# A two-layer graph network on one core: the second layer by node, the first layers a batch behind, and the last layers but one inside the last sums

## The chip, the cores and the metric

The kernel runs on one core of a Trainium2 chip. The metric is device time in microseconds (us) of one execution, the median of several runs. Five engines work side by side, each on its own queue of instructions: PE (TensorE, matrix products; PEld is its weight load), DVE (VectorE), ACT (ScalarE), POOL (GpSimd) and SP (SyncE, which here issues DMAs). In a product `matmul(ps, stationary, moving)` the stationary operand is loaded and the moving one is streamed through it. PSUM is the memory that PE writes to, in banks of 512 float32 columns; SBUF is the memory of the other engines. All waits between engines are semaphores that the framework's scheduler derives from the data.

## What is computed

There are 6250 nodes with 64 features, and 206250 directed edges (src, dst), sorted by dst: 100000 random pairs in both directions and a loop at each node. Cut to what matters:

```python
def gin_conv(x, Wa, ba, Wb, bb):
    h = x + segment_sum(x[src], dst, N)
    return relu(h @ Wa + ba) @ Wb + bb
def gnn0(h):                                   # 64 -> 128 -> 128, 128 -> 128 -> 64
    h = relu(gin_conv(h, W1, b1, W2, b2))
    return gin_conv(h, W3, b3, W4, b4)
def gnn1(h):
    y = mlp3(h[src], WM1, bM1, WM2, bM2, WM3, bM3)      # a message of each edge
    z = segment_sum(y, dst, N)
    return mlp3(concat([h, z]), WU1, bU1, WU2, bU2, WU3, bU3)
x = x + gnn0(maximum(layernorm(x), 0))
x = x + gnn1(maximum(layernorm(x), 0))
```

Messages depend on the source alone, so all three segment sums are products with one matrix A of edge counts, A[src, dst].

## The kernel before

The nodes are cut into 49 tiles of 128. The function `fast` (L152) has three stages.

**Stage 1, about 0 to 388 us: A is built, and the first sum is made beside it.** For each tile of destinations, `build` (L395) makes one-hot matrices of the tile's edges on DVE (`hot` L376: there L383, high L387, low L390), and PE multiplies them in four rounds of 16 products with 49 columns (cnt, L406). ACT takes each round from PSUM into `a` as counts (L408), and SP stores the tile to A in DRAM (L412). After each round, `build` calls `between(i)` (L533). That does a quarter of the first sum of the tile before (`FirstSum.quarter` L511: 49 products of 195 columns with the tile's counts as stationary and `hp`, the normalised nodes, as moving, L514, and one with the identity, L517). `hp` is kept as three bf16 parts of 64 features, and each part has one more column, of ones or zeros, whose sum counts the edges. A reduction on DVE (L520) adds the parts into `r1`.

`between` also runs what the table `beside` (L459 to L474) sets for this quarter: the preparation of later batches of edges. A batch has two chunks of edges; 13 batches cover the tiles, so one batch serves four tiles. The steps of a batch are `search_block` (ACT, L307, L309), `fetch_edges` (L312: DVE computes the addresses `off`, L318, and POOL issues the indirect DMAs d_win and s_win, L322), `fetch_blocks` (POOL, blk, L297), `slots` (L328, some ten small DVE operations on the lists, among them pair L341, mine L346, high_i L349), `cast` (ACT L364) and `turn` (PE L372, ACT L374).

After every fourth tile, `first_layers` (L523) copies the counted column to `sums` on POOL (L526) and calls `conv1` (L444) for the four tiles: `by_feature` (L415) splits r1 into two fp32r halves vr (ACT L251, DVE L252), turns them with four PE transposes tf (L421), and ACT brings them to f (L424). `layer` (L427) multiplies by the two halves of W1 (ps_t1, two products of 512 columns), ACT adds the bias and applies ReLU (t1, L433). The second layer is one fp32 product with w2 stationary and t1 moving (ps_t2, 512 columns), again with bias and ReLU on ACT. The features are on the partitions now, so four transposes tb (L450) bring the nodes back there, and `halves` writes h2r, the two fp32r halves of the hidden nodes (ACT L251, DVE L252). All pieces follow each other at once in the program, so PE meets each with as much other work between as the scheduler's order has placed.

The preparation of the edges runs up to four batches ahead. `follow` (L273) places an instruction behind the newest count on its engine without a wait.

**Stages 2 and 3, two calls of `sweep` (L620).** The groups are eleven of four tiles, one of three and one of two. For each group, SP loads A's columns in 13 chunks of four source tiles (a<-A, L629), DVE or ACT widens the bytes to fp32r (ar, L633), and PE sums over all 49 source tiles: in stage 2 two products for each (both halves of h2r, 98 in all, 512 columns), in stage 3 one (yr holds both halves). The layers that follow a group, conv2 (L592) and conv3 (L608), are called once the next group's sums have been issued (L642 to L644), and those of the last group after the loop (L645). `conv3` ends with o (L614) and its stores to the output (L617); the last group's output is two DMAs, a full tile and one of 106 rows, both on SP. `weight_halves` (L255) splits W1, WM1 and WU1 into fp32r halves after the second tile has been built (L546), all under one name.

The pools of stage 1 are closed at L552, and those of the sweeps (L553 to L557) take their place in memory.

Of the kernel before, what the change touches and what calls it, by code (L numbers as in the profile page):

```python
# [42 lines left out]
P = 128  # L43
N = 6250
E = 206250
D = 64
# [24 lines left out]
FIRST_HOTS = ((0, 16), (16, 16), (32, 32))  # L71
XT = 7
# [24 lines left out]
class Params:  # L97


    def __init__(self, nc, const, W1, b1, W2, b2, W3, b3, W4, b4,  # L100
# [31 lines left out]
        self.e1, self.e2, self.q3 = column(bU1, "e1"), column(bU2, "e2"), row(bU3, "q3")  # L132
        self.eps = const.tile([P, 1], FP, name="eps")
# [18 lines left out]
def fast(ctx: ExitStack, tc: tile.TileContext, x, src, dst, w, bad, out):  # L152
# [24 lines left out]
    w.load(nc.sync)  # L177

# [33 lines left out]
    D1 = D + 1  # L212
    hp = once.tile([P, NT, NP, D1], BF, name="hp")
# [8 lines left out]
    sums = const.tile([P, NT], FP, name="sums")  # L222

# [16 lines left out]
    def split(parts, v, n, f):  # L240

        p1, p2, p3 = (parts[:, :, i, :f] for i in range(NP))
# [12 lines left out]
    def weight_halves(w):  # L255

        t = const.tile([P, 1, 2, HID], FR, name="wp")
        follow(halves(t, w[:, None, :]), "ACT")
        return [t[:, 0, i, :] for i in range(2)]


    wins = building.enter_context(tc.tile_pool(name="f_wins", bufs=2))
    hots = building.enter_context(tc.tile_pool(name="f_hots", bufs=2))
    amat = building.enter_context(tc.tile_pool(name="f_amat", bufs=3))
# [150 lines left out]
    def by_feature(v, n, scale=1.0, to=None):  # L415

        vr = work.tile([P, 4, 2, D], FR, name="vr")[:, :n]
        halves(vr, v)
# [6 lines left out]
        return to  # L425

# [17 lines left out]
    def conv1(t, n, r):  # L444
        f = by_feature(r[:, :n, :D], n, UNIT)
        t1 = layer(w.c1, n, "t1", *((part, f) for part in w1p))
        t2 = layer(w.c2, n, "t2", (w.w2, t1))
        ps = bank("tb")
        for j in range(n):
            nc.tensor.transpose(ps[:, j * P:(j + 1) * P], t2[:, j * P:(j + 1) * P], w.ident)  # L450
        halves(h2r[:, t:t + n], ps[:, :n * P].rearrange("p (t f) -> p t f", f=HID))
# [23 lines left out]

    for b in range(4):
        search(b)
    for i in range(NP):
        nc.gpsimd.memset(hp[:, :, i, D:], 1.0 if i == 0 else 0.0)
# [22 lines left out]
    r1 = {}  # L502

    class FirstSum:


        def __init__(self, t, a):
            self.t, self.a = t, a.bitcast(F8)
            self.acc = pacc.tile([P, CH], FP, name="acc")[:, :NP * D1]

        def quarter(self, i):  # L511
            t = self.t
            for k in range((H * i + 3) // 4, (H * (i + 1) + 3) // 4):
                nc.tensor.matmul(self.acc, self.a[:, k, :], hp[:, k].rearrange("p i d -> p (i d)"),  # L514
                                 start=(k == 0), stop=False)
# [14 lines left out]
    for t in range(NT + 2):  # L530
# [19 lines left out]
        if t >= 2:  # L550
            first_layers(t - 2)
# [348 lines left out]
```

## Time and profile before

| | us |
|---|---|
| three runs | 938.75, 940.83, 939.69 (median 939.69) |
| the profiled execution | 936.85, its span 935.1, clock 0.99 |
| PE busy | 867.9 |
| DVE busy | 623.4 |
| ACT busy | 583.7 |
| POOL busy | 143.1 |

The profile is of one execution, slightly faster than the three timed runs. In its groups, `x2401 | 247.8, 251` means 2401 instructions, busy for 247.8 us together, with a mean of 251 ns for one; matmuls are pipelined and overlap each other, so on PE the time from one start to the next is what one costs, and the sum of durations is more than that. An fp32 product shows as two records (passes), an fp32r or bf16 product as one. `[2.44 <-DMA a<-A]` at the end of a line of the timeline is idle time of the engine before the instruction, and what ended it. In windows, the columns are the busy time (and the instructions) of PE, PEld, DVE, ACT and POOL, then the clock granted to PE, the share of the DMA engines and GB/s.

### The profile page before, as it was taken

Reading aid. Unit: us, or ns where it says so; the run is one execution under the profiler, and the core shown is the slowest. Engines: PE = TensorE matmul, PEld = TensorE weight load, DVE = VectorE, ACT = ScalarE, POOL = GpSimd, SP = SyncE. Lnnn points to the kernel's source line nnn. Section 1 sums busy time; section 2 is a strip of 40 time slices with the busy share of each in tenths; the row PEclk is TensorE's granted clock in tenths of the full one; section 3 lists DMA queues with packets and bytes.
Section 4 is the critical chain, followed back from the end, with each engine's and each line's share of the span. In section 5 each row is a group of like instructions: output and inputs, shape, how many; then the busy total and the mean of one; then the engine's idle time right before and its main releaser. Section 6 shows DMA issues by size and latency. Waiting matters only on the chain.

```text
span 935.1 us, 19639 instructions
## 1 busy us (share of the span) xinstructions
PE 867.9 (93%) x8225; PEld 732.1 (78%) x8225; DVE 623.4 (67%) x927; ACT 583.7 (62%) x757; POOL 143.1 (15%) x101
## 2 busy tenths in 40 slices
PE   0279999999999999899999999999999989999995
PEld 0179999999999999877777787777789757777784
DVE  6899988889998898544455554445545656665651
ACT  5967776777776666544545554544545857777762
POOL 3654333445332410000000000000000000000000
PEclk9989999999999999999999999999999989999998
DMA  6234333443423323655444444444434748887861
GB/s 133 82 133 169 148 136 140 156 160 138 169 114 123 145 105 127 195 139 142 113 115 120 123 105 123 118 114 116 111 92 121 208 135 225 224 228 209 239 180 47
DMA packets 195671, 133.71 MB, mean 143 GB/s; under 512 B 35220, under 2 KB 186900, under 8 KB 195572
## 3 DMA queue, kind: packets, MB, share of 16 engines
q1 hardware_dynamic: 189236, 121.34, 44.0%
q0 software_dynamic: 3600, 10.32, 3.6%
q8 instruction: 66, 1.08, 0.5%
q10 hardware_dynamic: 2736, 0.69, 0.3%
q14 instruction: 33, 0.27, 0.1%
HBM read 91.38 MB, written 40.94 MB: 142 GB/s over the span
## 4 chain that ended last, share of the span: by engine, by line
PE 81%; ACT 9%; DMA 4%; DVE 3%; issue 1%; SPq 0%; POOL 0%; ACTq 0%; DVEq 0%
PE acc L640 41%; PE acc L514 20%; PE ps_t L431 8%; PE cnt L406 6%; PE ps_y L440 4%; DMA a<-A 3%; ACT a L408 2%; ACT ar L633 2%; ACT t L433 2%; PE tf L421 1%; PE tb L450 1%; ACT blk L307 1%; ACT f L424 1%; ACT junk L287 1%; DMA xs<-in_x_dram 1%
## 5 line engine op out<-in xcount | busy, mean ns | idle before, releaser
L633 DVE CAST ar<-a 128x2048 fp32r<-128x2048 uint8 (+2 forms) x208 | 220.1, 1072 | 201.9 <-PE acc L640 160.0
L633 ACT CAST ar<-a 128x2048 fp32r<-128x2048 uint8 (+2 forms) x130 | 234.5, 1805 | 140.6 <-PE acc L640 121.9
L640 PE MATMUL acc<-ar,h2r 128*128 128x512 f32 (+2 forms) x1274 | 303.4, 391 | 2.4 <-DMA a<-A 2.4
L640 PEld LDWEIGHTS acc<-ar,h2r 128*128 128x128 f32 x1274 | 229.9, 188 | 56.7 <-issue 13.7
L514 PE MATMUL acc<-hp,a 128*128 128x195 bf16 x2401 | 247.8, 251 | 4.5 <-ACT a L408 2.9
L514 PEld LDWEIGHTS <-a 128*128 128x128 fp8e4 x2401 | 200.8, 99 | 12.5 <-issue 6.9
L408 ACT ACTIVATE a<-cnt 128x784 int16<-128x784 f32 x196 | 160.8, 821 | 68.7 <-PE cnt L406 67.6
L640 PE MATMUL acc<-ar,yr 128*128 128x512 f32 (+2 forms) x637 | 158.4, 400 | 0.1
L640 PEld LDWEIGHTS acc<-ar,yr 128*128 128x128 f32 x637 | 115.7, 189 | 32.9 <-issue 10.4
L406 PE MATMUL cnt<-high,low 128*128 128x49 bf16 x3136 | 114.9, 187 | 12.6 <-DVE low L390 11.1
L406 PEld LDWEIGHTS <-low 128*128 128x128 fp8e4 x3136 | 108.1, 97 | 17.2 <-DVE low L390 11.6
L390 DVE TENSOR_TENSOR low<-there,lkw 128x2048 int32<-128x2048 bf16 (+2 forms) x51 | 112.1, 2197 | 0.0
L387 DVE TENSOR_TENSOR high<-high,lkw 128x3136 bf16<-128x3136 bf16 (+2 forms) x51 | 87.6, 1719 | 5.2 <-PE cnt L406 5.0
L383 DVE TENSOR_TENSOR there<-word,lkw 128x2048 bf16<-128x2048 bf16 (+2 forms) x51 | 59.1, 1176 | 0.0
L297 POOL DMA_INDIRECT blk<-in_dst_dram,row x25 | 37.0, 1478 | 130.6 <-ACT junk L309 108.5
L322 POOL DMA_INDIRECT s_win<-in_src_dram,off x25 | 41.8, 1674 | 7.6 <-issue 7.3
L322 POOL DMA_INDIRECT d_win<-in_dst_dram,off x25 | 39.0, 1560 | 8.4 <-issue 5.8
L433 ACT ACTIVATE t<-ps_t,c 128x512 f32<-128x512 f32 (+3 forms) x39 | 25.9, 663 | 19.9 <-PE ps_t L431 18.7
L526 POOL COPY sums<-r 128x4 f32<-128x4 f32 (+1 forms) x13 | 22.7, 1743 | 101.0 <-DVE r L520 100.9
L372 PE MATMUL ps_win<-identb,parts 128*128 128x128 bf16 x75 | 8.9, 225 | 16.5 <-ACT parts L364 16.5
L433 ACT ACTIVATE t<-ps_t,d 128x512 f32<-128x512 f32 (+2 forms) x26 | 17.2, 662 | 11.0 <-PE ps_t L431 11.0
L520 DVE TENSOR_REDUCE r<-acc 128x65 f32<-128x195 f32 x49 | 17.3, 354 | 5.6 <-PE acc L517 5.6
(123 smaller groups left out, 618.0 us busy)
## 6 DMA issues: line engine op xcount, KB each, us to landing
a<-A SPq DMA_DIRECT2D x264, 256.0 KB, 3.1
A<-a SPq DMA_DIRECT2D x49, 784.0 KB, 3.5
a<-A SPq DMA_DIRECT2D x24, 192.0 KB, 2.6
a<-A SPq DMA_DIRECT2D x24, 128.0 KB, 2.2
a<-A SPq DMA_DIRECT2D x22, 64.0 KB, 2.2
out_dram<-o SPq DMA_DIRECT2D x11, 128.0 KB, 2.0
xs<-in_x_dram ACTq DMA_DIRECT2D x3, 224.0 KB, 5.5
xs<-in_x_dram SPq DMA_DIRECT2D x3, 224.0 KB, 6.1
```

What stands on the lines that cost most here:

```text
L322: nc.gpsimd.indirect_dma_start(out=win[:, i, :], out_offset=None, in_=of.rearrange("(a o) -> a o", o=1), in_offset=bass.IndirectOffsetOnAx ...
L383: nc.vector.tensor_tensor(there, word2[:, None, :, :].to_broadcast(shape), of(0)[:, :, None, :].to_broadcast(shape), op=OP.is_equal)
L387: nc.vector.tensor_tensor(high, high2[:, None, :, :].to_broadcast(shape), of(1)[:, :, None, :].to_broadcast(shape), op=OP.is_equal)
L390: counted["DVE"] = nc.vector.tensor_tensor(low.rearrange("p (g i) w -> p g i w", i=2), there.rearrange("p g w i -> p g i w"), of(2)[:, :, ...
L406: counted["PE"] = nc.tensor.matmul(ps[:, b, j * H:(j + 1) * H], low[:, g, :], high[:, g // 2, :, g % 2], start=True, stop=True)
L408: counted["ACT"] = nc.scalar.activation(a[:, :, k:k + 2 * PG].rearrange("p h (b j) -> p h b j", b=2), ps[:, :, :PG * H].rearrange("p b (j ...
L431: nc.tensor.matmul(ps[:, :n * P], wt, rhs, start=(i == 0), stop=(i == len(terms) - 1))
L433: nc.scalar.activation(to, ps[:, :n * P], AF.Relu, bias=bias)
L440: nc.tensor.matmul(ps[:, j * D:(j + 1) * D], lhs[:, j * P:(j + 1) * P], wt, start=True, stop=True)
L514: nc.tensor.matmul(self.acc, self.a[:, k, :], hp[:, k].rearrange("p i d -> p (i d)"), start=(k == 0), stop=False)
L633: widen(ar.rearrange(f"p k t b -> {order}"), a.rearrange(f"p t (k b) -> {order}", b=P))
L640: nc.tensor.matmul(acc[:, :n * P], part, ar[:, k - k0].rearrange("p t b -> p (t b)"), start=(k == 0 and i == 0), stop=(k == H - 1 and i == ...
```

## The change

Five things are edited.

1. *Second layer by node.* t1 is now the stationary operand, four times 128 columns, and w2 the moving one, so that the result has the nodes on the partitions. The bias is then along the columns, and a product of ones (2 x 128) with a row c2_r (2 x 512, the bias in two halves that add up) starts the sum in PSUM. ACT writes h2r's first half with a ReLU, DVE the second with a maximum and a difference. The transposes tb and the operation t2 are gone. c2_r takes one more DMA and some operations after the second tile.
2. *A batch behind.* `conv1` is split into first_halves, first_turn, first_layer and second_layer. These enter `beside`: in the second quarter of the tiles 4g+5, 4g+6 and 4g+7, with the second layer of the group before beside the first layer of the next. The last two groups, and group 10's second layer, follow the loop, interleaved.
3. *First sums.* `hp` has one column of ones for all parts, 193 columns in all, and two tiles share a PSUM bank. Both are reduced together after the second, and ACT, not POOL, takes `sums` from PSUM.
4. *Pools.* The pool of `a` is the first of the inner ones; the halves of W1 are in a pool of stage 1, those of WM1 and WU1 have names of their own.
5. *End.* In each sweep, the layers of the last group but one are called at the fifth chunk of the last group's sums. The last 106 output rows go out on ACT's queue.

```diff
+MIXED = (NT - 8) // 4 + 1
...
+    c2_row = once.tile([2, HID], FP, name="c2_row")
+    nc.sync.dma_start(c2_row, w.b2.rearrange("(o f) -> o f", o=1).broadcast_to([2, HID]))
...
-    D1 = D + 1
-    hp = once.tile([P, NT, NP, D1], BF, name="hp")
+    HP = NP * D + 1
+    hp = once.tile([P, NT, HP], BF, name="hp")
...
+    amat = building.enter_context(tc.tile_pool(name="f_amat", bufs=3))
     wins = building.enter_context(tc.tile_pool(name="f_wins", bufs=2))
     hots = building.enter_context(tc.tile_pool(name="f_hots", bufs=2))
-    amat = building.enter_context(tc.tile_pool(name="f_amat", bufs=3))
...
-    def conv1(t, n, r):
-        f = by_feature(r[:, :n, :D], n, UNIT)
-        t1 = layer(w.c1, n, "t1", *((part, f) for part in w1p))
-        t2 = layer(w.c2, n, "t2", (w.w2, t1))
-        ps = bank("tb")
+    def first_halves(g):
+        n = group(g)[1]
+        vr1[g] = work.tile([P, 4, 2, D], FR, name="vr")[:, :n]
+        follow(halves(vr1[g], r1[g][:, :n, :]), "ACT")
+
+    def first_turn(g):
+        f1[g] = turned(vr1.pop(g), group(g)[1], UNIT)
+
+    def first_layer(g):
+        f = f1.pop(g)
+        t1s[g] = layer(w.c1, group(g)[1], "t1", *((part, f) for part in w1p))
+
+    def second_layer(g):
+        t, n = group(g)
+        t1 = t1s.pop(g)
+        ps = bank("ps_h")
+        nc.tensor.matmul(ps[:, :n * HID], ones_r, c2_r[:, :n * HID], start=True, stop=False)
         for j in range(n):
-            nc.tensor.transpose(ps[:, j * P:(j + 1) * P], t2[:, j * P:(j + 1) * P], w.ident)
-        halves(h2r[:, t:t + n], ps[:, :n * P].rearrange("p (t f) -> p t f", f=HID))
+            nc.tensor.matmul(ps[:, j * HID:(j + 1) * HID], t1[:, j * P:(j + 1) * P], w.w2, start=False,
+                             stop=(j == n - 1))
+        v = ps[:, :n * HID].rearrange("p (t f) -> p t f", f=HID)
+        nc.scalar.activation(h2r[:, t:t + n, 0, :], v, AF.Relu)
+        nc.vector.scalar_tensor_tensor(h2r[:, t:t + n, 1, :], v, 0.0, h2r[:, t:t + n, 0, :],
+                                       op0=OP.max, op1=OP.subtract)
...
+    for g in range(MIXED):
+        for u, what, of in ((5, first_halves, g), (6, first_turn, g), (7, first_layer, g), (7, second_layer, g - 1)):
+            if of >= 0:
+                beside.setdefault(4 * (4 * g + u) + 1, []).append((what, (of,)))
...
-            self.acc = pacc.tile([P, CH], FP, name="acc")[:, :NP * D1]
+            if t % 2 == 0:
+                acc1[t // 2] = pacc.tile([P, CH], FP, name="acc")[:, :2 * HP].rearrange("p (t d) -> p t d", d=HP)
...
+                nc.tensor.matmul(acc[:, t % 2, :], ident_a, hp[:, t], start=False, stop=True)
+                if t % 2 == 1 or t == NT - 1:
+                    t0, n = t - t % 2, t % 2 + 1
+                    if t0 % 4 == 0:
+                        r1[t // 4] = work.tile([P, 4, D], FP, name="r1")
+                    for j in range(n):
+                        nc.vector.tensor_reduce(r1[t // 4][:, t0 % 4 + j, :],
+                                                acc[:, j, :NP * D].rearrange("p (k d) -> p d k", k=NP),
+                                                axis=AX.X, op=OP.add)
+                    follow(nc.scalar.copy(sums[:, t0:t0 + n], acc[:, :n, NP * D]), "ACT")
-
-    def first_layers(t):
-        if t % 4 == 3 or t == NT - 1:
-            t0, n = t - t % 4, t % 4 + 1
-            nc.gpsimd.tensor_copy(sums[:, t0:t0 + n], r1[t // 4][:, :n, D])
-            conv1(t0, n, r1[t // 4])
...
-                w1p, m1p, u1p = (weight_halves(x) for x in (w.w1x, w.m1x, w.u1x))
+                w1p = weight_halves(w.w1x, "w1p", once)
+                m1p, u1p = weight_halves(w.m1x, "m1p"), weight_halves(w.u1x, "u1p")
+
+                hi = once.tile([2, 2, HID], FR, name="c2_halves")
...
-        if t >= 2:
-            first_layers(t - 2)
+    for what, g in ((second_layer, MIXED - 1), (first_halves, MIXED), (first_turn, MIXED), (first_halves, MIXED + 1),
+                    (first_layer, MIXED), (first_turn, MIXED + 1), (second_layer, MIXED), (first_layer, MIXED + 1),
+                    (second_layer, MIXED + 1)):
+        what(g)
...
+                queue = nc.sync if m == P else nc.scalar
...
+                if (t, n) == GROUPS[-1] and c == 4:
+                    then(*pending)
+                    pending = None
```

`turned` is the second half of the old `by_feature`, from its transposes on.

## The prediction

> **What bounds the kernel now.** I read the page's busy rows first, then windows of 50 us, the timeline of each engine through one period of four tiles, DVE's waits, and both ends of the stages.
>
> ```profile
> PE 867.9 (93%) x8225; PEld 732.1 (78%) x8225; DVE 623.4 (67%) x927; ACT 583.7 (62%) x757; POOL 143.1 (15%) x101
> ```
> ```profile
> 200.00:250.00 50.00, 49.58 (x865) 46.81 (x864) 43.97 (x53) 35.73 (x57) 19.60 (x12) 1.00 0.37 140
> ```
>
> PE is the bound by the page. The window of stage 1 (columns: PE, PEld, DVE, ACT, POOL) says so too, but DVE is busy 43.97 of 50 there: two engines are near the end of their time. PE's timeline prices a first layer:
>
> ```profile
> 253.27 0.60 PE L421 MATMUL tf<-ident,vr 128*128 128x128 f32 x4
> ...
> 254.55 0.74 PE L431 MATMUL ps_t<-f,wp 128*128 128x512 f32 x2
> ...
> 256.07 1.13 PE L431 MATMUL ps_t<-t,w 128*128 128x512 f32 x2
> ...
> 257.97 0.66 PE L450 MATMUL tb<-ident,t 128*128 128x128 f32 x4
> ...
> 262.32 0.58 PE L406 MATMUL cnt<-high,low 128*128 128x49 bf16 x16
> ...
> 268.30 0.33 PE L372 MATMUL ps_win<-identb,parts 128*128 128x128 bf16 x3
> ```
>
> The tile that begins at 253.27 takes 9.05 us, the next, with no layers, 5.98: the layers cost PE 3.07 in each period. The ps_t with t as its moving operand, the second layer, comes at 90.70, 118.25 ... 311.28, so a period is 27.55 us.
>
> DVE's own loop is almost as long. Each period it sends out an address list (off), and later takes the gathered list (high_i):
>
> ```profile
> DVE high_i L349 <- DMA s_win<-in_src_dram,off: 20.1, 8, 3.9
> ```
> ```profile
> 224.44 0.15 DVE L318 TENSOR_SCALAR off<-off_f 128x2 int32<-128x2 f32 x1
> ...
> 235.26 0.29 DVE L349 TENSOR_SCALAR high_i<-s_win 128x256 int32<-128x256 int32 x1 [2.10 <-DMA s_win<-in_src_dram,off]
> ...
> 251.47 0.15 DVE L318 TENSOR_SCALAR off<-off_f 128x2 int32<-128x2 f32 x1
> ```
>
> From off to high_i it takes 10.84, 10.85, 10.69, 12.62, 10.82, 10.79, 11.92 and 11.34 in the eight periods (mean 11.23), each time with DVE idle at the end for the gather; from high_i to the next off it takes 16.21 where DVE waits for nothing. So DVE's loop is 16.21 + 10.8 = 27.0 at best, and 27.4 at the mean. PE can be given back only about half a microsecond per period before that loop is the bound.
>
> **Second layer by node (each number from PE's timeline, start to start).** Removed: the fp32 product of 512 columns (0.96), four tb (0.49), and the waits between the pieces (0.26 for f, 0.34 for t2; first layers a batch behind have nothing left to wait for). Kept: tf 0.45, ps_t1 0.47. Added: the bias product, one fp32r of 512 columns, 0.23 (the sums of stage 2 take 232.5 ns each), and four fp32 products of 128 columns with t1 stationary. No row has this product. Nearest are ps_y (x8 records of 64 columns, 114 ns start to start, 138 by duration) and the fp32 transposes (110 to 122 ns for 128 columns). Eight records at 114 to 138 give 0.91 to 1.10; I take 1.05, ends 0.95 and 1.35. Here a rule speaks against the change: the Trainium skill, "TensorE: Matmul & The Clock Gate", sections on LDWEIGHTS and on Weight-path perf modes, says that a load costs its columns over 1.2 ns, 128 columns some 107 ns, and that fp32 has no fast load, so eight loads alone would be 0.85, and with unhidden products of 53 to 60 ns behind them 1.3 (an estimate from that page). The ps_y row, which has the same loads, says they overlap; 1.35 stays the upper end. Sum: 0.45+0.47+0.05+0.23+1.05 = 2.25 against 3.07: -0.82 a group on PE (0.5 to 0.95). First sums of 193 columns in place of 195: 2 x 0.42 ns x 2450 = -2.0 us in all, at 86 ns each.
>
> **Does stage 1 get it?** In the order of instructions that DVE is given, its loop from high_i to off loses vr's second half (-0.34), gains a fourth reduce in that stretch (+0.27) and pair (+0.2): 16.34. With L from off to high_i as now (mean 11.23) the period is 27.57, with the shortest L 27.1; PE would like 27.55 - 0.82 - 0.17 = 26.56. So DVE and the gathers take the pace, and stage 1's period stays at 27.15 to 27.6. Would L shrink, as POOL loses its sums copy?
>
> ```profile
> 222.46 1.70 POOL L526 COPY sums<-r 128x4 f32<-128x4 f32 x1
> 224.32 1.05 POOL L297 DMA_INDIRECT blk<-in_dst_dram,row  x1 [0.16 <-issue]
> 225.68 1.06 POOL L322 DMA_INDIRECT d_win<-in_dst_dram,off  x1 [0.30 <-issue]
> 227.04 2.39 POOL L322 DMA_INDIRECT d_win<-in_dst_dram,off  x1 [0.30 <-issue]
> ```
>
> The second d_win takes 2.39 where the first takes 1.06, and it ends 0.82 after DVE's high (226.83, 1.78 long), as s_win ends 0.82 after low. The skill's "SBUF — State Buffer", Who interferes with whom, says that a DVE tensor_tensor has no mode that locks GpSimd out of writing descriptors; high and low are tensor_tensor, so by the rule POOL, 1.7 freer, would bring L to some 9.1, and PE would keep the pace. By the row the gathers end when high and low do, whatever came before: at 278.90, with no blk ahead of it, a d_win took 1.90 and L was 11.92. I go with the row: L stays.
>
> New waits: sums moves to ACT, behind DVE's two reduces, and queued behind it there are the second evacuation of cnt, a cast, t1 and h2r. The reduces come after DVE's high, so ACT, and PE behind its cnt bank, may stand until them: +0.2 to +1.5, once, since it delays PE against DVE and is then DVE's lead. The bias row's halves and the m1p/u1p splits go on DVE in the start, +1.9 us where DVE is busy 48.97 of the 50 us to 100; low is 1.4 us ahead of PE at 101, which takes up 0.8: +1.1. Gains of the period (0 to 0.4 x 8) against these: shift of PE at 323 us central +1.0, ends -6 (PE's pace) and +4. After 323 there are no gathers left and PE's saving counts: 2 groups x 0.82 and 10.8 tiles x 0.042, -2.1.
>
> **Between the stages.**
>
> ```profile
> 388.29 0.25 PE L517 MATMUL acc<-hp,ident_a 128*128 128x195 bf16 x1
> ...
> 391.41 0.94 PE L640 MATMUL acc<-ar,h2r 128*128 128x512 f32 x3 [2.44 <-DMA a<-A]
> ```
>
> From the last first sum to 403.15, when 36 sums are done, it takes 14.78: 36 x 0.2325 = 8.4, 3.2 of layers, 3.2 idle, 2.4 of it for a. In the new order SP has five loads ahead of the last stores of A, and the last layers interleave with the sums; PE has 8.4 + 4.4 of layers (group 10's second is now here): 12.85, so -1.9 (ends 0 and -3). Before stage 3, PE's order does not change; only u1p's split (0.2) leaves.
>
> **The end.**
>
> ```profile
> 914.98 1.10 PE L440 MATMUL ps_y<-u,t 128*128 128x64 f32 x8
> 915.89 4.44 PE L640 MATMUL acc<-ar,yr 128*128 128x256 f32 x35
> 920.17 0.51 PE L431 MATMUL ps_t<-h3f,wp 128*128 128x384 f32 x2
> ```
> ```profile
> 927.77 0.29 DVE L614 TENSOR_TENSOR o<-xs,ps_y 128x128 f32<-128x128 f32 x1 [2.91 <-PE ps_y L440]
> ```
> ```profile
> 928.09 1.36 SPq L617 DMA_DIRECT2D out_dram<-o  x2
> ```
>
> Both last layers follow the last sum, 7.6 us to o, with 2.5 us of PE waiting for ACT. With group 11's among the sums, its 2.5 us of products push the last sum to 922.7, and group 12's alone take 3.8 (924.27 to 927.77, and ps_y's wait): o at 926.5, -1.3 (ends -0.5, -2). The two output issues on one queue cost 1.36; on two, -0.4 (0 to -0.6).
>
> **Sum.** +1.0 - 2.1 - 1.9 - 0.2 - 1.3 - 0.4 = -4.9. The profiled execution took 936.85 (span 935.1), so 932.0; the median of the runs is 939.69, 2.84 above it: 934.8, say 935.0.
>
> **Rivals.** *PE keeps the pace (0.20):* L falls below 10.2 as POOL is freed. Then stage 1 gains -0.82 x 8 instead of +1.0: 924.4 profiled, 927. For it: the rule above; against it: gathers tied to high and low. *The list loop grows (0.20, slower):* in the stretch from off to high_i the gathers start straight after off, beside there and high, as at 278.90, and the store of A lies beside them. At L = 12.0, as the three longest average (12.62, 11.92, 11.34), the period is 28.3, +0.75 x 8 = +6, or 941; at 12.6 it is 28.9, +11, or 946: about 943.5. It decides from L = 11.2, and eats all the other savings from 11.8. For it: those three periods; against it: the first three, with sums and blk, were 10.8. *It does not do what it says (0.14):* the overlap at the transition is not had, as first loads still land late, and stage 1 only trades; the end alone remains: 938 to 940.
>
> **Numbers.** The likeliest case has 0.46, its own range 931.5 to 938.5. A measurement of this kernel can tell about 0.2%, 1.9 us. Faster: 0.40 of the likeliest, 0.20 of PE's pace, 0.04 of the last, 0.64. Slower: 0.16 of the list loop, 0.03 of the last, 0.19. The rest 0.17. The range of 926.5 to 942.5 leaves out half of PE's pace and the tail of the list loop.
>
> **What would show it.** Right: the second layer's eight records in about 1.05; period 27.1 to 27.6, with PE waiting for low and DVE for s_win; high_i less off near 10.8 to 11.2; first conv3 inside the last sums, o 3.8 after the last sum. Wrong: a period near 26.7 (PE's pace), or above 28 with L at 12; a new ACT wait for reduces in every period of over 1.5 us that shows as PE idle; a first load of a that still waits for a store.

## The result, and the profile after

The kernel after takes 939.18 us (median of 20 runs, 935.00 to 943.53), the kernel before in runs beside it 939.08 (20 runs, 936.91 to 941.35): ratio 1.000 (0.999 to 1.002). No difference can be measured. The profiled execution took 935.00 (span 933.2), the fastest of its 20; it is set here against the profiled one of before (span 935.1), and the 4 us between it and the median are taken up below. The experiments ran on several chips, and on three of these the kernel before takes 979 to 988 us in place of 938 to 940, so each is compared with the runs of before on its own chip; on the slower three these scatter from 971 to 991. Three of the six runs of after on one of the three were slow (958 to 961 at a granted clock of 0.97 to 0.98, the others 943 to 946 at 0.99) and are left out of its figures.

The busy row of the page, and the window of 50 us in stage 1 (PE, PEld, DVE, ACT, POOL, the clock granted to PE, DMA share, GB/s):

```profile
PE 864.7 (93%) x8261; PEld 737.7 (79%) x8261; DVE 624.4 (67%) x932; ACT 573.4 (61%) x770; POOL 125.3 (13%) x86
```
```profile
200.00:250.00 50.00, 47.04 (x805) 45.11 (x803) 41.81 (x52) 29.71 (x51) 16.60 (x10) 0.97 0.38 139
```

POOL and ACT are freer, as the change says. But PE is busy for 47.04 us of the window where it was 49.58 before, and its clock is 0.97: there is a new hole. First a period that has none, in PE's timeline:

```profile
149.56 0.60 PE L425 MATMUL tf<-ident,vr 128*128 128x128 f32 x4
149.99 0.58 PE L412 MATMUL cnt<-high,low 128*128 128x49 bf16 x16
...
155.88 0.72 PE L441 MATMUL ps_t<-f,w1p 128*128 128x512 f32 x2
156.53 0.49 PE L475 MATMUL ps_h<-c_r,ones_r 2*128 2x512 f32 x1
156.95 1.16 PE L477 MATMUL ps_h<-w,t 128*128 128x128 f32 x8
157.94 0.58 PE L412 MATMUL cnt<-high,low 128*128 128x49 bf16 x16
```

Start to start the eight records of the second layer take 0.99, the bias product 0.42, ps_t 0.65, tf 0.43: 2.49 a group, and PE waits for no other engine. The period, between the identity products at the end of tiles 12 and 16, is 26.79; it was 27.54. The period three further on is another matter. DVE, ACT and PE around its gather:

```profile
225.66 0.16 DVE L324 TENSOR_SCALAR off<-off_f 128x2 int32<-128x2 f32 x1
...
239.62 0.29 DVE L355 TENSOR_SCALAR high_i<-s_win 128x256 int32<-128x256 int32 x1 [5.36 <-DMA s_win<-in_src_dram,off]
239.82 1.78 DVE L393 TENSOR_TENSOR high<-high,lkw 128x3136 bf16<-128x3136 bf16 x1
241.53 0.61 DVE L560 TENSOR_REDUCE r<-acc 128x64 f32<-128x192 f32 x2
242.06 2.28 DVE L396 TENSOR_TENSOR low<-there,lkw 128x2048 int32<-128x2048 bf16 x1
```
```profile
242.17 0.16 ACT L563 COPY sums<-acc 128x2 f32<-128x2 f32 x1 [6.55 <-DVE r L560]
242.23 0.83 ACT L414 ACTIVATE a<-cnt 128x784 int16<-128x784 f32 x1
```
```profile
243.11 0.57 PE L412 MATMUL cnt<-high,low 128*128 128x49 bf16 x16 [2.64 <-ACT a L414]
243.53 1.50 PE L552 MATMUL acc<-hp,a 128*128 128x193 bf16 x12
```

The gathered list comes 13.96 after off, not 10.5; DVE stands 5.36 for it; ACT has the sums of two tiles to copy, which the reduces behind high_i must precede, and stands 6.55; the evacuation behind them is late, and PE stands 2.64 for its bank. Then the twelve sums take 1.50 where the same twelve take 1.19 in the clean period: in the 3.9 us after the wait the granted clock is 0.64. This period takes 31.12.

Two of the eight gathers are so late. In the eleven periods from tile 4 to tile 48, nine gained 0.2 to 1.65 (6.86 in all) and two lost 3.32 and 3.57 (6.89): 300.59 us against 300.57. At the last first sum PE is 2.0 later than before (390.30 against 388.29), which is what the start had cost by tile 4 (89.71 against 87.72).

The end is as foreseen. First PE's timeline (left out: the other pieces of the layers, and sums), then that of all engines from there on:

```profile
915.58 0.51 PE L441 MATMUL ps_t<-h3f,u1p 128*128 128x384 f32 x2
...
919.69 2.77 PE L695 MATMUL acc<-ar,yr 128*128 128x256 f32 x21
922.29 0.40 PE L441 MATMUL ps_t<-h3f,u1p 128*128 128x256 f32 x2
922.91 0.70 PE L441 MATMUL ps_t<-f,u1z 128*128 128x256 f32 x2 [0.23 <-ACT f L640]
924.18 0.70 PE L441 MATMUL ps_t<-t,u 128*128 128x256 f32 x2 [0.56 <-ACT t L443]
925.44 0.66 PE L450 MATMUL ps_y<-u,t 128*128 128x64 f32 x4 [0.56 <-ACT t L443]
```
```profile
926.14 0.29 DVE L665 TENSOR_TENSOR o<-xs,ps_y 128x128 f32<-128x128 f32 x1 [5.87 <-PE ps_y L450]
926.45 0.34 SPq L669 DMA_DIRECT2D out_dram<-o  x1
926.46 0.52 ACTq L669 DMA_DIRECT2D out_dram<-o  x1
```

o follows the last sum by 3.85, and the two output issues lie side by side.

### The profile page after: what moved, and what is told of

Same layout as the page of the kernel before. It is cut to its first block, busy times and chain, and to the rows that moved or that the text cites. A ratio compares the mean times of both kernels' runs of the same rounds, so it can differ in the third digit from the quotient of the medians.

```text
span 933.2 us, 19705 instructions
## 1 busy us (share of the span) xinstructions
PE 864.7 (93%) x8261; PEld 737.7 (79%) x8261; DVE 624.4 (67%) x932; ACT 573.4 (61%) x770; POOL 125.3 (13%) x86
## 4 chain that ended last, share of the span: by engine, by line
PE 60%; issue 18%; POOL 10%; DVE 6%; DMA 3%; ACT 2%; SPq 0%; POOLq 0%; DVEq 0%; ACTq 0%
PE acc L695 42%; PE ps_t L441 6%; PE acc L552 5%; POOL s_win L328 4%; PE ps_y L450 4%; POOL d_win L328 3%; POOL blk L303 3%; PE cnt L412 2%; DMA a<-A 1%; ACT ar L688 1%; PE tf L425 1%; DVE high L393 1%; DMA xs<-in_x_dram 1%; DMA s_win<-in_src_dram,off 1%; DVE low L396 1%
## 5 line engine op out<-in xcount | busy, mean ns | idle before, releaser
L695 PEld LDWEIGHTS acc<-ar,h2r 128*128 128x128 f32 x1274 | 230.1, 188 | 54.0 <-issue 10.5
L552 PE MATMUL acc<-hp,a 128*128 128x193 bf16 x2401 | 242.0, 251 | 4.3 <-DVE hp L253 2.8
L412 PEld LDWEIGHTS <-low 128*128 128x128 fp8e4 x3136 | 108.3, 97 | 22.2 <-DVE low L396 13.8
L303 POOL DMA_INDIRECT blk<-in_dst_dram,row x25 | 42.7, 1707 | 141.2 <-ACT junk L315 117.9
L563 ACT COPY sums<-acc 128x2 f32<-128x2 f32 (+1 forms) x25 | 4.0, 161 | 35.4 <-DVE r L560 35.3
L378 PEld LDWEIGHTS <-parts 128*128 128x128 bf16 x75 | 6.2, 102 | 19.4 <-ACT parts L370 19.4
L443 ACT ACTIVATE t<-ps_t,c 128x512 f32<-128x512 f32 (+3 forms) x26 | 17.4, 669 | 6.1 <-PE ps_t L441 6.1
```

Of the source, the lines that this page charges most:

```text
L303: nc.gpsimd.indirect_dma_start(out=blks[q], out_offset=None, in_=dst.rearrange("(r b) -> r b", b=BLK), in_offset=bass.IndirectOffsetOnAxis ...
L412: counted["PE"] = nc.tensor.matmul(ps[:, b, j * H:(j + 1) * H], low[:, g, :], high[:, g // 2, :, g % 2], start=True, stop=True)
L552: nc.tensor.matmul(acc[:, t % 2, :], self.a[:, k, :], hp[:, k], start=(k == 0), stop=False)
L695: nc.tensor.matmul(acc[:, :n * P], part, ar[:, k - k0].rearrange("p t b -> p (t b)"), start=(k == 0 and i == 0), stop=(k == H - 1 and i == ...
```

## Why a gather is late

Each tile's counts are stored to A by one DMA of 784 KB on SP, issued when the tile is done. The DMA part of the trace, from the end of GpSimd's last issue of s_win to high_i, in the late period (234.41 to 239.62), and then in the clean one (152.95 to 154.73). The first row is the share of the DMA engines in 40 slices; q1 carries the store, q0 the gather's transfers, q8 code:

```profile
DMA  0999949698909394929101011010101010000000
...
q1 hardware_dynamic: 144, 0.80, 41.3%
q0 software_dynamic: 32, 0.07, 3.2%
q8 instruction: 1, 0.02, 2.3%
```
```profile
DMA  0000000000000000909950390939999099990699
...
q1 hardware_dynamic: 52, 0.33, 43.6%
q0 software_dynamic: 32, 0.07, 20.4%
```

In the late period all 144 packets of the store run in the stretch that the gather is waited for. Cut into steps of 0.25 us, the same view has q1 alone from 234.50 to 236.75, and q0's packets in the step at 236.75 and after it; one more q0 packet comes at 238.75, behind a row of single q1 packets: in the step at 234.50 one packet of code had begun, which took 1.9 us (2.3% of 16 engines' time in 5.21 us). In the clean period q0 starts in the step at 153.50, and q1, in that at 153.75, is behind it. The store was issued 0.58 us before the end of GpSimd's last issue in the late period, and 0.05 before it in the clean one. All eight periods of after stand in one order: leads of 0.05, 0.06, 0.13 and 0.16 go with a landing 1.78 to 1.84 after GpSimd's issue, 0.25 and 0.30 with 2.60 and 2.56, 0.58 and 0.67 with 5.21 and 4.88. The last four have a packet of code beside them too, the first four none, so here the two causes come together: the store puts the bulk of the gather back by some 1.7 (q0 starts 2.4 after the end of the issue, not 0.7), and the code its last packet by another 2. In the kernel before the stores came 1.1 to 2.2 after the end of the gather's issue, and it landed in 1.48 to 1.64, save three periods (2.14 to 3.42) that each have a packet of code in the stretch.

The store gets ahead of the gather by the change itself, and in one step, by part 2. First before, then after, from the gather's last issue to the store (left out: all else):

```profile
142.84 0.25 PE L517 MATMUL acc<-hp,ident_a 128*128 128x195 bf16 x1
...
148.67 1.03 POOL L322 DMA_INDIRECT s_win<-in_src_dram,off  x1 [0.30 <-issue]
...
151.89 0.25 PE L517 MATMUL acc<-hp,ident_a 128*128 128x195 bf16 x1
151.90 0.32 SPq L412 DMA_DIRECT2D A<-a  x1
```
```profile
146.50 0.25 PE L554 MATMUL acc<-hp,ident_a 128*128 128x193 bf16 x1
...
151.72 1.23 POOL L328 DMA_INDIRECT s_win<-in_src_dram,off  x1 [0.30 <-issue]
...
152.88 0.25 PE L554 MATMUL acc<-hp,ident_a 128*128 128x193 bf16 x1
152.90 0.32 SPq L418 DMA_DIRECT2D A<-a  x1
```

In before, the first layers stand in the very tile whose end releases this store: from one identity product to the next it takes 9.05. In after only tf is left in it, the other products come in the tile behind, and it takes 6.38. So the store comes 8.7 after off where it came 11.4, while the end of GpSimd's last issue moved from 9.2 after off to 8.75 only; the lead of the first of the eight gathers is already 0.67. Within after, clean periods add to the lead slowly: PE's period is 26.78 and DVE's loop 16.33 + 10.55 = 26.88, so PE, and the store that waits for its counts, move ahead of the gather by some 0.1 per period (0.05, 0.13, 0.25), and by 0.33 where a packet of code holds DVE up, until the gather is late at 0.58; PE then loses more than DVE, and the lead is 0.06 again. That the step comes from part 2 is read from the two traces; no run puts the layers back into their tile.

## The experiments

**The kernel after once more.**

> The changed kernel once more, for a second profile. Theory (a late gather): in the first profile two of eight periods had the list s_win land 4.9 and 5.2 us after its issue instead of 1.8, and each of these two periods took PE some 4.3 us more than the 26.8 us of the others. So this profile again shows periods of 26.8 us and some of about 31, and its time is 926.5 + 4.2 for each late gather: 935 with two, 939 with three, 943 with four. Rival (a steady loss in every period): all periods alike, and the time within 1 us of the median 939.2 with no such steps.

Measured: 945.71 (943.3 to 946.4, three runs) where before takes 987.58, ratio 0.957 (0.953 to 0.961). All eight gathers were late here (off to high_i 11.85 to 13.8, periods of 28.2 to 30.2), so the mix of 26.8 and 31 that was expected did not come; PE stood 10.2 us for evacuations. On a chip where before takes 937.90:

> The changed kernel, once more. If this chip runs the kernel before in about 939: late gathers in two to four of eight periods, each with its store issued 0.5 us or more before the last gather of s_win ends on POOL, 935 to 943, about 10 above the kernel with its stores moved. If it runs it in about 980: late gathers in most periods, 940 to 960. Rival (the gather is late whenever it likes): late gathers also where the store is issued after the gather.

Measured: 937.80 (14 runs, 934.6 to 941.3), ratio 1.000 (0.998 to 1.001). The profiled run (938.49, span 936.7) again has eight late gathers, but by less: the store leads by 0.58 to 0.67 in each, the landing takes 3.1 to 4.3, off to high_i 11.85 to 13.04, a period 28.2 to 29.4. So runs differ in the pattern: two gathers late by 3.1 and 3.4 (935.0), or all late by some 1.7 (938.5). In two of the eight no packet of code lies in the stretch, and they landed after 3.10 and 3.14, where the clean periods of the first profile have 1.8: the store alone costs 1.3, and code beside it the rest. Which of the two a run falls into was not settled. The three traces have one thing in common: behind the two waits of PE after which the clock was lower (0.57 and 0.64, in the first profile) the lead fell to 0.05 and 0.06, and where the clock stayed at 1.00, in the other two, it stayed at 0.57 to 0.59.

**The store moved.** In `build`, `store()` issues the store of the tile before, which waits for the evacuation just made, the second of the next tile; no other engine's order changes (left out: the body of `store()`, and its call for the last tile).

```diff
-        nc.sync.dma_start(A[t], a.rearrange("p h g -> p (h g)").bitcast(U8))
+                if stores and k // (2 * PG) == 1:
+                    store()
+        stores.append((t, a))
...
```

> Alone the store of each tile of A is moved: it waits for the second evacuation of the next tile, some 3 us later. All engines' orders stay as in the changed kernel. Theory (the store, 784 KB, is issued 0.6 us before the last gather of s_win is, and the gather lands behind it): no gather later than about 2.6 us after its issue, no period over 27.5 us, median 926 to 931. Rival (gathers are late for a reason of their own): late gathers remain, 936 to 943. Rival (stores merely late for the buffers of a): slower than 943.

Measured: 930.36 (928.4 to 931.5) beside 987.58, ratio 0.943 (0.940 to 0.945). On a chip of the usual kind:

> The changed kernel with its stores moved, once more, as the base of the two runs beside it: 928 to 932, as the 930.4 before; every theory expects the same.

Measured: 928.10 (927.9 to 932.1) beside 939.89, ratio 0.989 (0.987 to 0.991). DVE's waits from 100 to 372 us and PE's from 40 to 400 (us in total, times, longest):

```profile
DVE high_i L355 <- DMA s_win<-in_src_dram,off: 17.9, 8, 3.1
```
```profile
PE cnt L422 <- ACT a L424: 1.9, 3, 1.2
```

In the kernel after these were 23.7 and 6.8. From tile 4 to tile 48 it takes 294.03, 6.56 less than after. Two periods over the expected 27.5 remain, of 28.04 and 27.57, whose gathers share the stretch with a packet of code. A third run asks whether distance matters, or only who comes first, with the store after the *first* evacuation, 0.85 to 1.15 behind the gather's issue:

> The kernel after, with the store of a tile's counts issued after the first (not the second) evacuation of the next tile, which is 0.9 to 1.5 us after the last list gather has left GpSimd in place of 5 to 6 us. Theory (a store costs something only when its transfers are in the DMA queues before those of the gather): off to high_i 10.3 to 11.7 in all eight periods, no wait of PE for a of more than 0.5 us in stage 1, 927 to 931. Rival (any store in flight beside the gather delays it, the lead does not matter): off to high_i 11.5 or more in several periods, and 932 to 938.

Measured: 927.99, ratio 0.987 (0.986 to 0.989). Off to high_i is 10.27 to 10.90, and 11.97 in one period, with a packet of code beside it. So who comes first decides: a store that follows the gather by 1 us costs no more than one that follows by 5.

**The same edit in the kernel before.**

> The kernel before with the stores of A alone moved, each behind the second evacuation of the next tile; all engines' orders stay. Theory (before is slowed here by the store beside the gather): period back to 27.5, median 938 to 945, and the kernel after with the same edit (930.4) stands 8 to 14 us below it, which is what the change is worth when no gather is late. Rival (before is slow here for another reason): within 5 us of the kernel before on this chip.

Measured: 984.01 beside 979.14, ratio 1.005 (1.003 to 1.007), with the stalls of the last section, so it tells little. And on a usual chip:

> The kernel before with its stores moved. Theory (the kernel before loses nothing to its stores, for they are issued 1 to 2 us after its gathers; and on a 980 chip its loss has to do with DVE's lead and not with stores): within 2 us of the kernel before on either kind of chip, so that the whole difference to the changed kernel with its stores moved, 11 us, is the change's own. Rival (stores cost both kernels alike): 5 us or more faster than the kernel before.

Measured: 944.23 beside 937.90, ratio 1.006 (1.003 to 1.008): slower by 6, and the expectation failed. The trace shows why. In before the stores were behind the gathers already; moved, the store of the tile before falls 2.1 to 2.5 ahead of the end of GpSimd's last issue. DVE's wait for the list grew from 20.1 to 25.5 in all, and in a late period (178.35, at the end of GpSimd's issue, to 181.68, high_i) the stretch holds store and gather together, and no code:

```profile
q1 hardware_dynamic: 68, 0.33, 29.1%
q0 software_dynamic: 64, 0.13, 11.9%
```

Two of the eight still landed in 1.70 and 1.75: their store led by 2.54 and was nearly over (24 and 25 of its 144 packets were left). So the same edit helps after and harms before, and both by where it puts the store against the gather.

**Lists a quarter earlier.** The steps of a batch from the search on are set one quarter of a tile earlier.

```diff
-            at(10 + 2 * i, search_block, b + 3, i)
-        at(13, fetch_edges, b + 3)
-        at(14, fetch_blocks, b + 4)
+            at(9 + 2 * i, search_block, b + 3, i)
+        at(12, fetch_edges, b + 3)
+        at(13, fetch_blocks, b + 4)
```

> The changed kernel with search_block, fetch_edges and fetch_blocks one quarter of a tile, 1.5 us, earlier in the table. Theory (gathers that are sent 1.5 us sooner land before the store is issued): gathers land 1.6 to 2.6 us after their issue, no period over 27.5, 927 to 934. Rival (gathers are late whatever lies beside them): as the changed kernel, 940 to 955 on this chip.

Measured: 939.42 beside 979.14, ratio 0.956 (0.952 to 0.960). Off to high_i is 9.0 to 9.7 in five periods and 12.0 to 13.9 in three. In the five the store follows GpSimd's issue by 1.3 to 1.5, in the three it leads by 0.6. The edit moved the meeting and did not end it.

**The sums on DVE.** Is the wait of ACT a price of its own?

```diff
-                    follow(nc.scalar.copy(sums[:, t0:t0 + n], acc[:, :n, NP * D]), "ACT")
+                    follow(nc.vector.tensor_copy(sums[:, t0:t0 + n], acc[:, :n, NP * D]), "DVE")
```

> The changed kernel with the copy of sums on DVE, right behind the two reduces, in place of ACT. Gathers are as late as ever; what changes is that ACT no longer stands behind the reduces with the next evacuation of cnt. Theory (a late gather costs PE 1 to 2.6 us through ACT and the rest through low): no wait of PE's cnt for ACT in the tile after high_i, 0.5 to 2.5 us less for each late gather, so some 4 to 12 us below the changed kernel on the same chip. Rival (low is what comes last anyway): within 2 us of the changed kernel.

Measured: 950.11 beside 979.14, ratio 0.969 (0.965 to 0.973), with stalls of another kind (last section): it tells nothing. On a usual chip:

> The kernel after, with the copy of the sums on DVE behind the reduces instead of on ACT; the stores of A are left where they are. The run of this kernel before this one had stalls on PE of another kind, so it told nothing. Theory (the late gather is the cost, and ACT's wait only the way by which it reaches PE): ACT no longer waits for the reduces, but where a gather lands late PE waits for DVE's low at the next tile by about as much, and the time stays at 935 to 942. Rival (the wait of ACT is itself the price, and without it PE runs on): waits of PE of at most 1 us in each period, 929 to 934.

Measured: 928.87 (922.2 to 929.6), ratio 0.986 (0.982 to 0.990), the rival's range. But not for the rival's reason. One gather was as late as in after (off to high_i 12.93), and PE's timeline there reads

```profile
240.68 0.59 PE L412 MATMUL cnt<-high,low 128*128 128x49 bf16 x16 [2.44 <-DVE low L396]
```

so PE stands 2.44 for low where it stood 2.64 for a, and that period takes 30.93 against 31.12. In this one period at least ACT's wait was the way, not the price. The gain is elsewhere: with the copy on DVE the scheduler also puts `there` behind `mine`, and GpSimd ends its last issue 7.7 after off, not 8.75. Four more gathers land late (3.0 to 3.8 after that end), and the time won covers it: the mean from off to high_i is 10.76, not 11.56, and tile 4 to tile 48 takes 296.19, not 300.59.

Both edits together:

> The kernel after with both edits: the sums copied by DVE, and the store of a tile issued after the next tile's first evacuation. Theory: with the order of DVE that comes with the copy the last list gather is issued 7.7 us after off in place of 8.75, as in the run with that edit alone, and with the stores moved it lands undisturbed, 1.6 to 1.8 us later (3 where a code load lies beside it): off to high_i 9.3 to 10.7 in all eight periods. DVE's loop is then 16.45 + 9.3 = 25.8, below PE's 26.78, so a period stays at 26.78 and only the one of 28.1 that the run with the stores moved still had goes: 924 to 927. Rival (PE's own pace is all there is to be had, and the later stores now meet other transfers, the loads of blk or d_win): 927.5 to 931.

Measured: 967.17 beside 985.32, ratio 0.983 (0.979 to 0.986), with PE standing 12.1 us between 150 and 300 us for nothing that the trace shows. It failed, and on the usual kind of chip the pair was not tried.

**No wait for the list.** In after and in before, high_i and word are kept behind the newest count on DVE (left out: the same edit at word):

```diff
-        nc.vector.tensor_scalar(high, s, 7, 63, op0=OP.logical_shift_right, op1=OP.bitwise_and)
+        follow(nc.vector.tensor_scalar(high, s, 7, 63, op0=OP.logical_shift_right, op1=OP.bitwise_and), "DVE")
```

> Alone high_i and word of the next lists are kept behind the count of the tile at which their slots stand, some 14 us later in DVE's order, so that DVE no longer stands waiting for the gather just sent. Theory (late gathers reach PE only because DVE waits for them in order): DVE has no wait for s_win, all periods at PE's own 26.8 us, median 925 to 930. Rival (the new wait of ACT for the two reduces, whatever the gather does): ACT still holds the count's bank, 934 to 942. Rival (period bound by DVE's own work): periods of over 27.3, 932 to 938.

> The same pin of high_i and word in the kernel before. Theory (PE sets its pace at 27.55 us and its lead of 1.5 us covers the wait for the gather): within 2 us of 939.1, period 27.5. Rival (DVE's loop with its wait of 2 to 4 us was the bound already): 933 or less, period under 27.2.

Measured beside 987.58: after 962.27, ratio 0.976 (0.973 to 0.979), before 984.18, 1.002 (0.999 to 1.005). DVE's wait went, as meant, and periods became about 32 by the stalls of the last section. A miss, which tells nothing of the gathers. Before as it is, on such a chip:

> The kernel before, profiled on the chip of these experiments, where its runs took 987.6 us in place of 939. Theory (the phase of the store against the gather): its start is some 5 us later here, and so the store of A meets the gather of s_win in each period; periods of 30 us or more in stage 1 in place of 27.55, stages 2 and 3 as before. Rival (all of this chip is slower): the sweeps are longer too, or the clock is lower.

Measured: 979.47. Off to high_i is 11.2 to 12.0, and in six of the eight periods DVE stands 0.03 for the list, so the store was not what slowed before there; DVE's other stretch is 21 to 22 in those six in place of 16.2, since DVE waits for PE (19.1 us for cnt alone). To make DVE's loop the longer one, `there` is computed four times in every fourth tile of before, from tile 12 on (left out: where `times` is set):

```diff
-        nc.vector.tensor_tensor(there, word2[:, None, :, :].to_broadcast(shape),
-                                of(0)[:, :, None, :].to_broadcast(shape), op=OP.is_equal)
+        for again in range(times):
+            nc.vector.tensor_tensor(there, word2[:, None, :, :].to_broadcast(shape),
+                                    of(0)[:, :, None, :].to_broadcast(shape), op=OP.is_equal)
```

> The kernel before with more work on DVE: for every fourth tile from the twelfth on, there is written four times over instead of once, 3.5 us more of DVE in a period; nothing else. Theory (on this kind of chip DVE gets ahead, its high waits for PE's cnt, POOL then sends its gathers back to back beside an idle DVE, PE's issue stalls in that time, its clock is halved and PE falls further behind): a busier DVE stays behind PE, the gathers lie beside its work, the clock stays at 1.0, and the kernel is faster by 20 us or more, 945 to 965. Rival (PE is late for a reason that has nothing to do with DVE's lead): the same or slower, 980 to 1000.

> The kernel before with 3.5 us more of DVE work in each period of four tiles. If this chip runs the kernel before in about 939: as before, 940 to 943 with a uniform period of 28.1. If it runs it in about 980, theory (DVE's lead brings the loss): 945 to 965, with the clock at 1.0 through stage 1; rival (the loss has another cause): 980 to 1000.

Measured on usual chips: 941.76, ratio 1.002 (1.001 to 1.003), and 940.97, 1.003 (1.002 to 1.004). The period is 28.13 with no wait for the list: 3.5 us more on DVE cost 0.6 in a period, since the wait for the list (2.5 at the mean) had covered most of it. On the other chips it was not tried.

**The parts of the change, on the kernel with the stores moved.** Without part 5:

```diff
-                queue = nc.sync if m == P else nc.scalar
+                queue = nc.sync
...
-                if (t, n) == GROUPS[-1] and c == 4:
-                    then(*pending)
-                    pending = None
```

> The same without the change's end: the last layers but one follow the last sums again, and all output goes out on SP's queue. Theory (the end was worth what the first profile shows, 1.1 us at o and 0.3 in the output): 1.0 to 1.8 us above the base. Rival (the extra products only push the last sum, and nothing is won): within 0.4 us of the base.

Measured: 929.77 (927.1 to 935.9), ratio to before 0.990 (0.987 to 0.992): 1.7 above 928.10, which these few runs do not separate (927.9 to 932.1 there). The profiles differ by 2.3, of which 0.9 lies ahead of the end; from conv3's first ps_t of group 10 to the end of the span it is 24.25 against 22.80, so the end is worth some 1.4, as expected. With the second layer by feature again at the new places (the bias row, then without use, is left out):

```diff
-        nc.tensor.matmul(ps[:, :n * HID], ones_r, c2_r[:, :n * HID], start=True, stop=False)
...
+        t2 = layer(w.c2, n, "t2", (w.w2, t1))
+        ps = bank("tb")
         for j in range(n):
...
+            nc.tensor.transpose(ps[:, j * P:(j + 1) * P], t2[:, j * P:(j + 1) * P], w.ident)
+        halves(h2r[:, t:t + n], ps[:, :n * P].rearrange("p (t f) -> p t f", f=HID))
```

> The same with the second layer as before, by feature: one fp32 product of 512 columns, bias and ReLU on ACT, four transposes tb, halves; it keeps its place a batch behind, and the bias row and its operations are left out. Theory (PE keeps the pace once no gather is late, and the new second layer is 1.4 us of PE in place of 0.96 + 0.49 and the wait of 0.3 for t2): 3 to 8 us above the base. Rival (DVE's loop with its gathers keeps the pace even then, as predicted): within 2 us of the base.

Measured: 944.67, ratio to before 1.005 (1.004 to 1.006): 16.6 more than 928.10, twice the most that was expected. PE's waits from 100 to 372 us:

```profile
PE tb L487 <- ACT t L453: 16.4, 8, 2.9
```

tb waits for t2, and ACT's t2 now stands behind the copy of the sums, which waits for the reduces: 2.0 in each of eight periods. The layer by node has no such step between its two products and its result. So nearly all of the 16.6 is this wait, and not PE's own work.

## Why the prediction was wrong

The forecast was a gain of 4.9; the profiled pair has 1.9, and the medians none. In the first profile of after the last first sum comes 2.0 later than before, in the one of 938.49 it is 6.3 later; the forecast had 1.1 earlier. Step by step:

*Second layer by node, -0.82 a group.* The eight records: 0.99 against 1.05, so loads overlap products, as the ps_y row said, and the upper end of 1.35, in which they do not, was not met. The bias product 0.42 against 0.23, ps_t 0.65 against 0.47: PEld stands 0.37 and 0.24 before the loads of the bias product and of the first of the eight (156.53, 156.95), so these two loads are not covered. So -0.58; with the shorter sums (-0.17) it makes -0.75, and the clean period is 0.77 shorter.

*"DVE and the gathers take the pace, and stage 1's period stays at 27.15 to 27.6."* DVE's stretch was 16.33 against 16.34, exactly. **"L stays" is the step that failed.** L was taken as the mean of before (11.23) or its best (10.8). Undisturbed it is 10.5 to 10.6, and the clean period 26.78, better than foreseen. But L depends on where the store lies, and the change moved the store: with the layers gone from its tile it is issued 2.7 earlier after off, ahead of the gather. The eight L of after have a mean of 11.56, and those of the run of 938.49 one of 12.3. With the stores behind the gather it is 10.7 and 10.8, and the time 928. The rival "the list loop grows" named the cause, "the store of A lies beside them", and gave it 0.20 and a size of 12.0 to 12.6; the profiles have 11.56 and 12.3. It took the three long gathers of before for a sign of it, though, and by before's trace these had their store 1.6 to 2.2 behind them and a packet of code beside them. What the prediction lacked was a check that it could have made: the stores' issues in before's trace stand 1.1 to 2.2 behind the gathers', and taking 3.07 of layers out of the tile between uses that up. The likeliest case put this move of the store at nothing.

*New waits: ACT behind the reduces, "+0.2 to +1.5, once".* It was 2.4 and 2.6, in two periods, and as the way of the late gather. The two periods came out 4.1 and 4.3 longer (30.89 and 31.12 against 26.78), the wait and what the lower clock behind it took. Start: by tile 4 PE is 2.0 later, not 1.1, as if nothing of the 1.9 on DVE had been covered.

*First transition -1.9:* -0.6 (14.0 from the last first sum to the end of 36 sums, against 14.6). The prediction's 14.78 goes to 403.15, when 37 sums are done; 36 are done at 402.9. The wait for a is gone, as foreseen; the products are slower than counted, with ten sums between the layers taking 0.30 each, not 0.2325, and layers of 4.9, not 4.4. (One more reading is off by 0.1: the second layers start at 90.60, 118.15 ... 311.18. The period is the same.)

*End -1.3, output -0.4:* -1.1 from ps_t's place to o (-0.5 at conv3's ps_t of group 10 against -1.6 at o), and -0.2 from o to the end of the span: right in mechanism, and some 1.4 by the experiment. Stage 3's sums before it came out 2.0 shorter between the two profiled runs, with nothing in the change to explain it. From its first sum to that ps_t stage 3 takes 181.9 to 184.4 over the profiles of after and its variants on usual chips, so this lies within the scatter, and the 1.9 of the profiled pair rests on it.

Without the meeting the change is worth what the clean periods say: 928.0 and 928.1 against 939.3 and 939.9, 1.3% and 1.1%, beyond the prediction's likeliest and close to the rival of PE's pace (927), though not for that rival's reason: the clean L is 10.5, not below 10.2. The best version on the usual chips is the kernel after with its stores behind the gathers; with the sums on DVE (928.87) it is as fast within the scatter.

The Trainium skill, "DMA: Bandwidth & Descriptors", Queues, rings and completion order, says that a DMA engine takes turns between its queues and drains a whole packet, typically 9 to 17 descriptors, before it changes over. The store has nine records for each engine (144 over 16). If each record is such a packet, the gather should lose about two of them, half a microsecond (an estimate: 0.24 each, from the 41.3%); if the nine are the descriptors of one packet, it should stand behind all nine. The trace has it behind the whole store, 1.7 later than in the clean period. That fits the second reading; no view here tells a packet from a descriptor.

## What to carry to other kernels

When a change speeds one engine, or moves its work from one tile to another, list the DMAs whose issue is tied to that engine and see which transfers on another engine's short path they will now run ahead of; the margin is in the trace of before as two issue times (here 1.1 to 2.2, against 2.7 by which the store moved). A gather that ends a loop should be issued before, not after, a bulk store, and moving a store is a change of its own whose sign depends on the place it came from.

## What the hardware showed that was not expected

PE's clock fell after waits of 2.41 and 2.64 us in after, 2.44 with the sums on DVE, and 2.04 and 2.66 with the layer by feature (granted 0.57 to 0.66 in the next 4 us), but stayed at 1.00 after waits of 2.47 and 2.51 in after on a slower chip, 2.44 in before (391.41) and 2.88 with the layer by feature. The skill's "TensorE: Matmul & The Clock Gate", Part 1, has an idle window of about 3.4 us that runs free of the kernel. That the same length of wait goes either way fits a free-running window; that 2.0 can be enough fits a whole idle window less well.

One packet of code (0.02 MB) took 0.9 to 1.9 us of a DMA engine, and in six periods in which one met a gather that no store led (three of before, three of after with the stores moved) the gather landed 2.1 to 3.4 after its issue, not 1.5 to 1.8.

On the chips where before takes 979 to 988, PE's products come in bursts with gaps that no semaphore ends, here in the run of before on such a chip:

```profile
160.93 0.30 PE L406 MATMUL cnt<-high,low 128*128 128x49 bf16 x5 [0.24 <-issue]
161.66 0.29 PE L406 MATMUL cnt<-high,low 128*128 128x49 bf16 x5 [0.43 <-issue]
162.38 0.26 PE L406 MATMUL cnt<-high,low 128*128 128x49 bf16 x4 [0.44 <-issue]
```

A burst of five every 0.72 us, and the clock halved behind it (0.50 from 164 to 170), once in most periods. On these chips it came in before, with its stores moved too, in both kernels without a wait for the list, and where the sums are on DVE, but not in after as it is (945.71), hardly with its lists earlier (three gaps), and not with its stores moved alone (930.36 there, 928.10 elsewhere). In the runs that have it DVE is ahead of PE: in before there it waits 5.4 us for the list in all, not 20.1. Whether that is the cause stays open.
